# Two strides of the third attention, the opening of a 30-step FFN, and the order and register loads of an expert stage

## The chip, the cores and the metric

The kernel runs on one core of a Trainium2 chip. The metric is the time of one execution on the device in microseconds (us), as the median of several runs. Five engines work side by side, each through its own list of instructions: PE (matrix products), DVE and POOL (elementwise, POOL also sends gathers and scatters), ACT (functions of one operand), and SP, which only issues transfers (DMA). Instructions wait for one another by semaphores.

## What is computed

The input x has 4096 rows of 256 values, adj is a 4096 x 4096 matrix of zeros and ones. Two layers follow one another, each a graph attention and then a network on the rows, with residual additions. Cut to what matters:

```python
# attention, 4 heads of 64; W, a1, a2 differ by layer
h = einsum('nd,mdo->mno', x, W)
e = leaky_relu((h @ a1)[:, :, None] + (h @ a2)[:, None, :], 0.2)
attn = softmax(where(adj > 0, e, -9e15))
out = elu(attn @ h)                      # heads side by side

# layer 0
x = x + attention(layernorm(x))                          # g0
def step(h):                                             # 30 times
    h = h + 0.01 * tanh(h)
    h = h * sigmoid(h)
    return layernorm(h) @ W.T + b
x = x + thirty_steps(layernorm(x))
# layer 1
x = x + attention(attention(layernorm(x)))               # g1, then g2
f = layernorm(x)
p = softmax(relu(f @ rw1 + rb1) @ rw2 + rb2)             # 6 experts
weights, which = softmax(top 2 of p), their numbers
expert(e) = relu(relu(f @ w1[e] + b1[e]) @ w2[e] + b2[e]) @ w3[e] + b3[e]
x = x + sum of weights * expert(which)
```

## The kernel before

A group is 4 tiles of 128 rows: 8 groups of 512 rows in all (G = 4, NG = 8). The stages follow one another; in the profiled execution g0 ends near 603 us, the FFN near 1627, g1 at 2109 and g2 at 2646, and then come the experts.

**Attention** (`attention`, from L161). A stage first prepares: it loads the rows by groups (`load`, L258; the four buffers `ring` are shared between stages through `load_ahead`, L90), transposes them (`columns`, L268), multiplies by the weights (`products`, L297), and splits the values h into a high and a low f16 half in `vals` (`upper`, L364, on ACT; `lower`, L382, on DVE). g2 takes its rows without normalising them; there POOL spreads the rows' sums `xt` over 128 columns (`xsb`, L431 and L432) as the left side of a product on PE. Then the main part runs over chunks of 8 tiles of rows, heads, and quarters of the other rows. `step_of` (L450) makes signs `st` by ACT (L464) or DVE (L462), and DVE makes two masks of them with the loaded mask `m` (L569, L575). PE multiplies each mask by a row of 130 values (L521, in `products`, L509). The list of DVE and ACT is written out by hand there. Sums are closed by `lower_sums` (L470), `whole_sums` (L476) and `close` (L480). The last argument of `attention`, `apart`, holds two strides in elements: from one row of values in `vals` to the next (f16), and between two sums in PSUM (f32, `apart_s`):

```python
acc[:, i, part * apart_s : part * apart_s + 2 * DV],
masked[part][:, at_i // TR, s, rows],
values[:, j, h, part],
```

DV is 65. g0 has (130, 130), g1 (160, 130), g2 (130, 256), set in the calls (L1011).

**FFN** (L828 to L982). A unit is one group in one of 30 steps, 240 units in all. `slot(at)` (L857) issues parts of several units: tanh (L907) on ACT and the addition (L908) on POOL of unit `at`; silu (L893), the f16 half (L897, ACT) and the other half (`lower`, L898, DVE) of unit `at` − 2, with a transposing DMA of both halves issued by SP; statistics (L917, L919) on DVE; transposes on PE and a copy (L924) of unit `at` − 3, its deviation (L927 on ACT, L928 on POOL); the products (L937, L940) of unit `at` − 4, and scaling (L877) by DVE of unit `at` − 5. The lists of PE, DVE, ACT and POOL are in the order in which the code issues them, SP's is not: a scheduler places its transfers. The table `opening` adds, in the first slots, the normalisation of the first rows: `measure` (L747, DVE), `rate` (L755: ACT, then POOL at L760, L762 and L763), and `init` (L774), which normalises a group either on ACT (L782) or, with its third argument True, on DVE (L779). From slot 32 on, the rows of the residual are loaded again, a group each 24 slots (`load` into `ring`, `load_apart` into `hold`, L835), since the last step adds them.

**Experts** (from L1018). The 4096 rows are treated as two halves. `route` (L1080) is a generator with six parts for one half: for each group statistics (`over_std`, L96: L101 and L103 on DVE, L105, and a power on POOL at L106), normalisation `n` (L1111, L1114), a store of `n` to `nd`, transposes (L1122), the router's product (L1101), its second product (L1131) and logits; then the two best experts; then the place of each row in a list sorted by expert, from which come `expert` (the expert's number of each of T = 37 tiles, L1240 to L1248), `source` and `dest` (L1250 to L1260; the sums by PE at L1231), the biases `bsel` (L1263 to L1273), and the weights of the two experts. Half 0 is routed ahead of the loop; after its first four parts the experts' weights `ew` (18 x 256 KB) and `b3` are loaded. The loop (L1419 on) takes the 74 tiles one after another: `gather` (L1312) fetches the rows by `source` four tiles ahead, `turn` transposes them (L1326, L1328), `fetch` (L1330) copies an expert's weights (L1346), `hidden` (L1348: products L1354, L1365 on ACT, L1367 on DVE) runs twice, `result` (L1369: products L1375, addition and scatter to `yd`, L1378). Half 1 is routed in parts between the tiles. `combine` (L1390) loads the results of a half and adds them, weighted, to `acc`, from where they are stored.

The number of the expert is an address in three engines. `fetch` reads it into registers of PE, DVE and ACT, for a few tiles at a time:

```python
n = min(4, T - t)
_, values = nc.values_load_multi_w_load_instructions(
    expert[h][0:1, t : t + n],
```

Of the kernel before, what the change touches and what calls it, by code (L numbers as in the profile page):

```python
# [11 lines left out]
F32 = mybir.dt.float32  # L12
# [6 lines left out]
OP = mybir.AluOpType  # L19
AX = mybir.AxisListType  # L20
# [3 lines left out]
P = 128  # L24
C = 256
KC = C // P
H = 4
D = C // H
E = 6
G = 4  # L30
# [4 lines left out]
DV = D + 1  # L35
# [11 lines left out]
def gnn_ffn_kernel(ctx: ExitStack, tc: tile.TileContext, a: dict, out: bass.AP):  # L47
# [34 lines left out]
    def rows_of(t, g):  # L82
        return t[g * GR : (g + 1) * GR, :].rearrange("(r p) c -> p r c", p=P)
# [6 lines left out]
    def load_ahead(src, g, view=rows_of, queue=nc.sync):  # L90
        t = ring[:, turns[0] % 4]
        turns[0] += 1
        queue.dma_start(t, view(src, g))
        ahead[g] = t

    def over_std(pool, src):  # L96

        st = pool.tile([P, G, 6], F32, name="ln_st")
        mv = pool.tile([P, G, 2], F32, name="ln_mv")
        for r in range(G):  # L100
            nc.vector.bn_stats(st[:, r, :], src[:, r, :])  # L101
        for r in range(G):
            nc.vector.bn_aggr(mv[:, r, :], st[:, r, :])  # L103
        rstd = pool.tile([P, G], F32, name="ln_rstd")
        nc.vector.tensor_scalar(rstd, mv[:, :, 1], EPS, None, op0=OP.add)  # L105
        nc.gpsimd.tensor_tensor(rstd, rstd, mhalf, OP.pow)  # L106
        return rstd, mv
# [53 lines left out]
    def attention(tag, src, norm, w, front, chunks, first, ends, following, side={}, apart=(2 * DV, 2 * DV)):  # L161
# [7 lines left out]
        with ExitStack() as scope:  # L169
# [68 lines left out]
            with ExitStack() as ps:  # L238
# [189 lines left out]
                if sums is None:  # L428
                    xt = prep.tile([P, KC], F32, name="xt")
                    nc.vector.tensor_reduce(xt, xs, axis=AX.X, op=OP.add)  # L430
                    xsb = prep.tile([P, KC, P], F32, name="xsb")  # L431
                    nc.gpsimd.tensor_copy(xsb, xt[:, :, None].to_broadcast([P, KC, P]))  # L432
                    pt = small_ps()
                    for k in range(KC):
                        nc.tensor.matmul(pt[:, :C], xsb[:, k, :], w[:, k, :C], start=(k == 0), stop=(k == KC - 1))
                nc.scalar.activation(
# [304 lines left out]

    def load(g, queue=nc.sync):
        if g not in ahead:
            load_ahead(x1d, g, queue=queue)
        x1[g] = ahead.pop(g)

    def measure(g):  # L747
# [79 lines left out]
    with ExitStack() as scope:  # L827
# [7 lines left out]
        def load_apart(src, g):  # L835
            x1[g] = hold.tile([P, G, C], F32, name="x1")
            nc.sync.dma_start(x1[g], rows_of(src, g))

        for g in range(4, NG):
# [5 lines left out]

        th, zs, mvs, rs, zT, zT16, pos = {}, {}, {}, {}, {}, {}, {}
        units = FFN_STEPS * NG
        opening = {
            0: [(init, 2)],
            1: [(rate, 4), (rate, 5), (init, 3, True)],  # L850
            2: [(init, 4, True)],
            3: [(init, 5, True), (measure, 6)],
            4: [(rate, 6), (measure, 7)],
            5: [(init, 6), (rate, 7)],
            6: [(init, 7)],
        }
        def slot(at):  # L857
            g, part = divmod(at - 4 * NG, 3 * NG)
            if 0 <= g < NG and part == 0:
                if g < NG // 2:  # L860
                    load(g)
                else:
                    load_apart(x1d, g)
            u = at - 3
# [26 lines left out]
            if 0 <= u < units:  # L891
                z = zs[u] = work.tile([P, G, C], F32, name="z")
                ins = nc.scalar.activation(z, th.pop(u), AF.Silu, scale=0.01)  # L893
                if not u:
                    follows(ins, closed[1], "one change of tables")
                z16 = work.tile([P, 2, G, P], F16, name="z16", bufs=4)
                nc.scalar.activation(z16[:, 0], z[:, :, P:], AF.Identity, scale=scale[:, :1])  # L897
                lower = nc.vector.scalar_tensor_tensor(  # L898
                    z16[:, 1], z[:, :, P:], scale[:, :1], z16[:, 0], op0=OP.mult, op1=OP.subtract
                )  # L900
                zT16[u] = work.tile([P, 2 * G, P], F16, name="zT16", bufs=4)
                nc.sync.dma_start_transpose(zT16[u], z16.rearrange("p s r c -> p (s r c)"))
# [83 lines left out]
    def runs_of(t, g):  # L986

        return t[g * GR : (g + 1) * GR, :].rearrange("(p r) c -> p r c", r=G)
# [11 lines left out]
    for n in range(2):  # L1000
# [10 lines left out]
            {} if n else side,  # L1011
            (2 * DV, 256) if n else (160, 2 * DV),
        )
# [7 lines left out]
    with ExitStack() as scope:  # L1021
# [3 lines left out]
        bT = one.tile([P, NB], F32, name="bT")  # L1025
        acc = one.tile([P, NT, C], F32, name="acc")
        ws = one.tile([P, 2, NT], F32, name="ws")
        bsel = [one.tile([P, T, 2 * KC], F32, name=f"bsel{h}") for h in range(2)]
        expert = [one.tile([P, T], I32, name=f"expert{h}") for h in range(2)]
        dest = [one.tile([P, T], I32, name=f"dest{h}") for h in range(2)]  # L1030
        source = [one.tile([P, T], I32, name=f"source{h}") for h in range(2)]
        ew = [one.tile([P, E, KC, C], F32, name=f"ew{i}") for i in range(3)]
        b3 = one.tile([P, E, C], F32, name="b3")
# [43 lines left out]
        def over(t, n=NTH, m=E):  # L1077
            return t[:, :, None].to_broadcast([P, n, m])

        def route(h, turned, bank):  # L1080

# [3 lines left out]
            def load(g):  # L1085
                if h * NGH + g not in ahead:
                    load_ahead(x3d, h * NGH + g, runs_of)
                rows[g] = ahead.pop(h * NGH + g)

            load(0)  # L1090
            load(1)
            for g in range(NGH + 2):
                if g + 2 < NGH:
                    load(g + 2)
                if g < NGH:
                    stds[g] = over_std(rwork, rows[g])
# [8 lines left out]
                if 1 <= g <= NGH:  # L1105
# [18 lines left out]
                    nc.scalar.activation(acc[:, at : at + G, :], t, AF.Identity, bias=mone)  # L1124
                    yield
                if 2 <= g:
                    u = g - 2
# [91 lines left out]
            for i in range(2):  # L1219
# [18 lines left out]
                yield  # L1238
            seen = rone.tile([P, T, E - 1], F32, name="seen")
            nc.vector.tensor_tensor(  # L1240
                seen,
                along[:, :T, None].to_broadcast([P, T, E - 1]),
                first[:, None, 1:].to_broadcast([P, T, E - 1]),
                OP.is_ge,
            )
            ex = rone.tile([P, T], F32, name="ex")
            nc.vector.tensor_reduce(ex, seen, axis=AX.X, op=OP.add)
            nc.vector.tensor_copy(expert[h], ex)  # L1248
            lst = rone.tile([P, T, 2], F32, name="lst")
# [10 lines left out]
            nc.vector.tensor_copy(dest[h], df)  # L1260
            yield
            ohe = rone.tile([P, T, E], F32, name="ohe")
            nc.vector.tensor_tensor(  # L1263
# [19 lines left out]
        with tc.tile_pool(name="r_ps", bufs=1, space=PSUM) as psum, tc.tile_pool(  # L1283
# [7 lines left out]
            nc.tensor.transpose(ps[:, :NB], br, ident[:NB, :NB])  # L1291
            nc.vector.tensor_copy(bT, ps[:, :NB])
            steps = route(0, turned, bank)
            for _ in range(4):
                next(steps)
            for i in range(3):
# [3 lines left out]
            nc.sync.dma_start(b3, bcast_rows(a["L1_ffn_expert_b3"]))  # L1300
            for _ in steps:
                pass

# [26 lines left out]
        def fetch(i):  # L1330

            h, t = divmod(i, T)
            if i not in which:
                n = min(4, T - t)
                _, values = nc.values_load_multi_w_load_instructions(
# [135 lines left out]
```

## Time and profile before

| | us |
|---|---|
| median of 3 runs | 2967.96 (2966.99 to 2968.54) |
| the profiled execution | 2983.79 |
| its span | 2982.0 |
| PE busy in the span | 2795.9 (94%) |
| DVE busy | 2737.1 (92%) |
| ACT busy | 2463.9 (83%) |
| POOL busy | 1159.1 (39%) |

All durations come from the one profiled execution, whose time stands beside the median. A row of the groups gives a line of the code, its engine and operation, what it writes and reads, the shapes, the number of instructions; then the busy time in us and the mean of one in ns; then the engine's idle time just ahead of such instructions and what ended most of it. In a timeline each row is a start, a duration, the engine, the line and the operation; x4 stands for four in a row, and brackets hold the idle time before it. The clock in the windows is the share of full speed that PE was granted.

### The profile page before, as it was taken

The page shows a single profiled execution, that of the slowest core. Times are in us where ns is not written, and L with a number is a line of the kernel's source. Part 1 is how long each engine was busy: PE and PEld are TensorE (multiplying, and loading weights), DVE is VectorE, ACT ScalarE, POOL GpSimd, SP SyncE. Part 2 cuts the span into 40 slices and gives each one's busy share as a digit, 9 for nine tenths or more (in the row PEclk, how much of TensorE's full clock was granted, in tenths as well). Part 3 has the DMA queues.
Part 4 walks back from the last instruction along what each step waited for, and adds up shares of the span by engine and source line. Part 5 has one row for each costly group of instructions (what it writes and reads, how often), then busy time and mean ns, then how long its engine had stood idle before and what let it go on. Part 6 is the DMA issues. An engine that isn't in the chain of part 4 may idle for free. (4 is left out here: it accounts for less than half of the span.)

```text
span 2982.0 us, 82665 instructions
## 1 busy us (share of the span) xinstructions
PE 2795.9 (94%) x33923; PEld 2553.5 (86%) x33923; DVE 2737.1 (92%) x5769; ACT 2463.9 (83%) x3125; POOL 1159.1 (39%) x1084
## 2 busy tenths in 40 slices
PE   7899999979999999999998999999899999977986
PEld 5799999968888888888887999999799999967885
DVE  7999999999999999999998899999889999976665
ACT  5799999978888888888877999999799999954332
POOL 3000000079999999999982000000300000015563
PEclk9999999989999999999999999999999999988998
DMA  9999885043333333333353032120302222142243
GB/s 281 274 258 242 230 234 159 25 126 69 68 69 68 68 67 70 68 67 70 68 110 119 26 99 72 49 87 27 108 27 94 66 94 94 31 141 93 79 165 133
DMA packets 484450, 320.07 MB, mean 107 GB/s; under 512 B 416589, under 2 KB 445418, under 8 KB 477930
## 3 DMA queue, kind: packets, MB, share of 16 engines
q1 hardware_dynamic: 474034, 290.27, 36.1%
q0 software_dynamic: 7104, 19.41, 2.1%
q8 instruction: 268, 4.39, 0.6%
q10 hardware_dynamic: 2936, 5.11, 0.5%
q14 instruction: 108, 0.88, 0.1%
HBM read 183.00 MB, written 52.04 MB: 79 GB/s over the span
## 5 line engine op out<-in xcount | busy, mean ns | idle before, releaser
L521 PE MATMUL acc<-vals,st 128*128 128x130 f16 x12288 | 1425.1, 219 | 39.0 <-DVE u L476 30.6
L521 PE MATMUL acc<-vals,below 128*128 128x130 f16 x12288 | 1424.7, 221 | 14.0 <-DVE below L575 13.2
L464 ACT ACTIVATE st<-f1b,nf 128x1024 int8<-128x1024 f32 x1265 | 1334.2, 1145 | 30.3 <-PE acc L521 19.8
L521 PEld LDWEIGHTS <-below 128*128 128x128 fp8e4 x12288 | 1185.9, 97 | 55.0 <-issue 42.6
L521 PEld LDWEIGHTS <-st 128*128 128x128 fp8e4 x12288 | 1207.2, 98 | 9.6 <-DVE st L569 7.8
L937 PE MATMUL po<-wT,zT 128*128 128x256 f32 x1920 | 576.2, 382 | 6.1 <-DVE y L877 3.5
L940 PE MATMUL po<-w,zT 128*128 128x256 f16 x3840 | 577.9, 273 | 0.5 <-DMA zT<-z 0.5
L908 POOL TENSOR_TENSOR th<-th,y 128x1024 f32<-128x1024 f32 x232 | 548.9, 2366 | 14.5 <-DVE z_st L917 0.4
L940 PEld LDWEIGHTS <-zT 128*128 128x128 f16 x3840 | 376.6, 98 | 161.7 <-DMA zT<-z 1.2
L575 DVE TENSOR_TENSOR below<-m,st 128x1024 int32<-128x1024 int32 x384 | 469.9, 1224 | 32.6 <-DVE st L569 0.9
L569 DVE TENSOR_TENSOR st<-st,m 128x1024 int32<-128x1024 int32 x384 | 466.8, 1216 | 0.2
L877 DVE SCALAR_TENSOR_TENSOR y<-po,z_rs,bias 128x256 f32<-128x256 f32 x928 | 384.3, 476 | 2.2 <-PE tp L869 0.7
L917 DVE BATCH_NORM_STATS2 z_st<-z 128x6 f32<-128x256 f32 x960 | 335.5, 412 | 0.0
L937 PEld LDWEIGHTS po<-wT,zT 128*128 128x128 f32 x1920 | 291.1, 192 | 15.6 <-issue 3.7
L893 ACT ACTIVATE z<-th 128x1024 f32<-128x1024 f32 x240 | 251.9, 1050 | 17.6 <-POOL th L908 16.8
L928 POOL TENSOR_TENSOR z_rs<-z_rs,mhalf 128x4 f32<-128x4 f32 x240 | 245.4, 1022 | 3.1 <-ACT z_rs L927 3.1
L907 ACT ACTIVATE th<-y 128x1024 f32<-128x1024 f32 x232 | 241.7, 1042 | 0.0
L924 ACT COPY zT<-tp 128x512 f32<-128x512 f32 x240 | 140.4, 585 | 90.6 <-PE tp L869 89.5
L462 DVE TENSOR_SCALAR st<-f1b,nf 128x1024 int8<-128x1024 f32 x271 | 201.0, 742 | 6.2 <-PE acc L521 6.2
L760 POOL TENSOR_TENSOR x_rs<-x_rs,mhalf 128x4 f32<-128x4 f32 x8 | 9.4, 1175 | 505.3 <-ACT x_rs L759 505.3
L1046 POOL IOTA along_i<- 128x512 int32 (+1 forms) x5 | 2.8, 557 | 485.8 <-PE acc L521 485.7
L439 POOL MEMSET hs<- 128x4 f32 x3 | 0.3, 103 | 485.9 <-DVE u L493 485.9
(263 smaller groups left out, 3158.5 us busy)
## 6 DMA issues: line engine op xcount, KB each, us to landing
ring<-in_adj_dram SPq DMA_DIRECT2D x64, 1024.0 KB
m<-edges SPq DMA_DIRECT2D x32, 1024.0 KB
f1b<-fd SPq DMA_DIRECT2D x48, 512.0 KB
edges<-m SPq DMA_DIRECT2D x16, 1024.0 KB
y<-yd SPq DMA_DIRECT2D x16, 512.0 KB
ew<-in_L_ffn_expert_w_dram SPq DMA_DIRECT2D x18, 256.0 KB
t<-in_x_dram SPq DMA_DIRECT2D x8, 512.0 KB
old<-in_x_dram SPq DMA_DIRECT2D x16, 256.0 KB
```

Of the source, the lines that this page charges most:

```text
L464: nc.scalar.activation(out, f1, AF.Sign, bias=f2, scale=-1.0)
L521: nc.tensor.matmul(acc[:, i, part * apart_s : part * apart_s + 2 * DV], masked[part][:, at_i // TR, s, rows], values[:, j, h, part], start ...
L569: nc.vector.tensor_tensor(above, above, whole, OP.bitwise_and)
L575: nc.vector.tensor_tensor(below, whole, above, OP.bitwise_xor)
L877: nc.vector.scalar_tensor_tensor(t[:, r, :] if end else y[:, g * G + r, :], po[:, r, :], rstd[:, r : r + 1], t[:, r, :] if end else bias, ...
L893: ins = nc.scalar.activation(z, th.pop(u), AF.Silu, scale=0.01)
L907: nc.scalar.activation(th[at], was, AF.Tanh, scale=0.01)
L908: ins = (nc.gpsimd if at else nc.vector).tensor_tensor(th[at], th[at], was, OP.add)
L917: nc.vector.bn_stats(st[:, r, :], z[:, r, :])
L928: nc.gpsimd.tensor_tensor(rs[u], rs[u], mhalf, OP.pow)
L937: nc.tensor.matmul(po[:, r, :], src[:, r * P : (r + 1) * P], wT, start=True, stop=False)
L940: nc.tensor.matmul(po[:, r, :], src16[:, part * G + r, :], w16[:, other, :], start=False, stop=(part == 1 and other == 1),)
```

## The change

It has six parts.

1. g2 gets the strides of g1, (160, 130). Its `xsb` is dropped: PE reads `xt` itself, spread by the access pattern.
2. In the FFN's opening, groups 4 and 5 are normalised on ACT, not on DVE, in slots 3 and 4; group 3 stays on DVE. The rates of groups 4 and 5 are issued in slot 0, not in slot 1.
3. The eight loads of rows for the residual each get a dependence on the latest `lower` (L898), so that the scheduler can't place them earlier.
4. In the experts' stage, the rows of half 1 are loaded straight into `acc`, the first two groups ahead of the weights, and the statistics of these two groups are issued within the routing of half 0. `expert` is worked out after `source` and `dest`. DVE's list in the routing of half 0 is in the order of the code.
5. `ew` is allocated in the reverse order, ahead of `acc` and `ws`.
6. An expert's numbers are read in three loads for each half: 4, 17 and 16 tiles; before there were ten.

The diff, cut to its core:

```diff
@@ over_std, attention, load
-    def over_std(pool, src):
+    def over_std(pool, src, mark=""):
...
-                    xsb = prep.tile([P, KC, P], F32, name="xsb")
-                    nc.gpsimd.tensor_copy(xsb, xt[:, :, None].to_broadcast([P, KC, P]))
                     pt = small_ps()
                     for k in range(KC):
-                        nc.tensor.matmul(pt[:, :C], xsb[:, k, :], w[:, k, :C], start=(k == 0), stop=(k == KC - 1))
+                        nc.tensor.matmul(
+                            pt[:, :C], xt[:, k : k + 1].to_broadcast([P, P]), w[:, k, :C], start=(k == 0), stop=(k == KC - 1)
+                        )
@@ the FFN
+        halved = []
         opening = {
-            0: [(init, 2)],
-            1: [(rate, 4), (rate, 5), (init, 3, True)],
-            2: [(init, 4, True)],
-            3: [(init, 5, True), (measure, 6)],
-            4: [(rate, 6), (measure, 7)],
-            5: [(init, 6), (rate, 7)],
+            0: [(init, 2), (rate, 4), (rate, 5)],
+            1: [(init, 3, True)],
+            3: [(init, 4), (measure, 6)],
+            4: [(rate, 6), (init, 5), (measure, 7)],
+            5: [(rate, 7), (init, 6)],
             6: [(init, 7)],
         }
...
-                if g < NG // 2:
-                    load(g)
-                else:
-                    load_apart(x1d, g)
+                ins = load(g) if g < NG // 2 else load_apart(x1d, g)
+                follows(ins, halved[0], "in mid-stage, when the queue has room")
...
+                halved[:] = [lower]
@@ the call for g1 and g2
-            (2 * DV, 256) if n else (160, 2 * DV),
+            (160, 2 * DV),
@@ the experts
-        acc = one.tile([P, NT, C], F32, name="acc")
-        ws = one.tile([P, 2, NT], F32, name="ws")
...
-        ew = [one.tile([P, E, KC, C], F32, name=f"ew{i}") for i in range(3)]
+        ew = [one.tile([P, E, KC, C], F32, name=f"ew{i}") for i in (2, 1, 0)][::-1]
+        acc = one.tile([P, NT, C], F32, name="acc")
+        ws = one.tile([P, 2, NT], F32, name="ws")
...
+        early = {}
+
+        def rest(g):
+            return acc[:, (NGH + g) * G : (NGH + g + 1) * G, :]
+
+        def measure_other(g):
+            early[g] = over_std(rone, rest(g), f"_{g}")
@@ route
             def load(g):
-                if h * NGH + g not in ahead:
-                    load_ahead(x3d, h * NGH + g, runs_of)
-                rows[g] = ahead.pop(h * NGH + g)
+                if h:
+                    rows[g] = rest(g)
+                    if g in early:
+                        stds[g] = early.pop(g)
+                    else:
+                        nc.sync.dma_start(rows[g], runs_of(x3d, NGH + g))
+                else:
+                    rows[g] = ahead.pop(g)
...
-                if g < NGH:
+                if g < NGH and g not in stds:
                     stds[g] = over_std(rwork, rows[g])
...
+                if not h and g >= NGH:
+                    measure_other(g - NGH)
...
-            seen = rone.tile([P, T, E - 1], F32, name="seen")
-            nc.vector.tensor_tensor(
-                seen,
-                along[:, :T, None].to_broadcast([P, T, E - 1]),
-                first[:, None, 1:].to_broadcast([P, T, E - 1]),
-                OP.is_ge,
-            )
-            ex = rone.tile([P, T], F32, name="ex")
-            nc.vector.tensor_reduce(ex, seen, axis=AX.X, op=OP.add)
-            nc.vector.tensor_copy(expert[h], ex)
             lst = rone.tile([P, T, 2], F32, name="lst")
...
             nc.vector.tensor_scalar(source[h], sf, float(NH - 1), None, op0=OP.min)
             nc.vector.tensor_copy(dest[h], df)
             yield
+            seen = rone.tile([P, T, E - 1], F32, name="seen")
+            nc.vector.tensor_tensor(
+                seen,
+                along[:, :T, None].to_broadcast([P, T, E - 1]),
+                first[:, None, 1:].to_broadcast([P, T, E - 1]),
+                OP.is_ge,
+            )
+            ex = rone.tile([P, T], F32, name="ex")
+            nc.vector.tensor_reduce(ex, seen, axis=AX.X, op=OP.add)
+            nc.vector.tensor_copy(expert[h], ex)
@@ around route(0)
+            for g in range(2):
+                nc.sync.dma_start(rest(g), runs_of(x3d, NGH + g))
             steps = route(0, turned, bank)
-            for _ in range(4):
-                next(steps)
+            with tc.manual_schedule(engines={mybir.EngineType.DVE}):
+                for _ in range(4):
+                    next(steps)
...
-            for _ in steps:
-                pass
+            with tc.manual_schedule(engines={mybir.EngineType.DVE}):
+                for _ in steps:
+                    pass
@@ fetch
-                n = min(4, T - t)
+                n = 4 if t == 0 else min(-(-(T - 4) // 2), T - t)
```

## The prediction

> **What bounds the kernel now.** I read the page first, for the costliest groups and the slices; then busy time by windows, to cut the span into stages; then, in each stage that the change touches, the timeline and the waits. The edits lie in four places: the third attention (g2), the opening of the FFN (603 to 650 us), the head of the experts' stage (2646 to 2704 us) and its loop (2704 to 2957 us).
>
> ```profile
> L521 PE MATMUL acc<-vals,st 128*128 128x130 f16 x12288 | 1425.1, 219 | 39.0 <-DVE u L476 30.6
> ```
>
> The attentions are bound by PE: a row of this kind stands twice, and only 39.0 us of idle time precede 1425 us of work. Cut by attention (g0, g1, g2 in order; columns: window, its length, PE busy and matmuls, PEld busy, clock, DMA share, GB/s):
>
> ```profile
> 100.00:600.00 500.00, 476.52 (x8108) 471.07 (x8106) 0.99 0.72 198
> 1640.00:2105.00 465.00, 458.13 (x8030) 455.57 (x8028) 1.00 0.18 58
> 2170.00:2640.00 470.00, 465.61 (x8037) 463.65 (x8035) 1.00 0.21 65
> ```
>
> A matmul takes 458.13/8030 = 57.05 ns in g1 and 465.61/8037 = 57.93 ns in g2, at the same clock, shape and type. What differs in the code between the two is the pair of strides, and g2's masks and values lie elsewhere.
>
> In the FFN DVE sets the pace, 3.8 us per unit from 646 us on (37.99 busy of 38). In its opening DVE normalises rows:
>
> ```profile
> 610.66 0.69 DVE L628 SCALAR_TENSOR_TENSOR e<-e,u 128x512 f32<-128x512 f32 x1
> 611.46 3.42 DVE L779 TENSOR_SCALAR ring<-ring,x_rs,x_nm 128x256 f32<-128x256 f32 x4
> ...
> 617.05 3.37 DVE L779 TENSOR_SCALAR x<-x,x_rs,x_nm 128x256 f32<-128x256 f32 x4
> ```
>
> Four of these operations take 3.4 us here, while POOL adds (L908, below); the same shape at L1114 takes 0.41 each.
>
> ```profile
> 614.04 1.08 POOL L760 TENSOR_TENSOR x_rs<-x_rs,mhalf 128x4 f32<-128x4 f32 x1
> ...
> 617.49 2.47 POOL L908 TENSOR_TENSOR th<-th,ring 128x1024 f32<-128x1024 f32 x1
> ```
>
> In the head DVE works without a break from the logits to `source`, and PE waits:
>
> ```profile
> 2684.20 0.25 DVE L1201 TENSOR_TENSOR at__45084<-ps_s,shift 128x96 f32<-128x96 f32 x1
> ...
> 2685.72 1.07 DVE L1267 TENSOR_TENSOR sel<-ohe,bT 128x888 f32<-128x888 f32 x1
> ...
> 2688.70 0.77 DVE L1221 TENSOR_TENSOR ohh<-along,hi 128x592 f32<-128x592 f16 x1
> ...
> 2694.04 1.40 DVE L101 BATCH_NORM_STATS2 ln_st<-ring 128x6 f32<-128x256 f32 x4
> 2695.36 0.22 DVE L1250 COPY lst<-ps_r 128x74 f32<-128x74 f32 x1
> ...
> 2697.09 0.17 DVE L1259 TENSOR_SCALAR source<-sf 128x37 int32<-128x37 f32 x1
> ```
>
> The gather that needs `source` then stands behind one more operation of POOL:
>
> ```profile
> 2696.88 1.01 POOL L106 TENSOR_TENSOR ln_rstd<-ln_rstd,mhalf 128x4 f32<-128x4 f32 x1 [33.16 <-DVE sf L1258]
> 2698.15 1.54 POOL L1315 DMA_INDIRECT gx<-nd,source  x1 [0.26 <-DVE ln_mv L103]
> ```
>
> After that PE leads (window, length, PE busy, PEld, DVE, ACT, POOL, clock, DMA share, GB/s):
>
> ```profile
> 2640.00:2704.00 64.00, 29.00 (x236) 21.13 (x234) 43.84 (x159) 19.14 (x28) 19.85 (x38) 0.71 0.52 179
> 2704.00:2860.00 156.00, 148.77 (x1084) 136.60 (x1083) 101.99 (x321) 62.34 (x147) 92.32 (x92) 0.98 0.33 110
> ```
>
> **The change, part by part.** The sums are against the profiled run: 2983.79 us, a span of 2982.0 and 1.8 around it. It is 15.8 above the median of 2967.96; I carry the difference in us over to the median unchanged.
>
> *Strides of g2.* They become those of g1. By the busy times the gain is 0.88 ns x 8192 matmuls = 7.2 us; by the starts of g1's and g2's matmuls outside stalls (57.6 against 56.7 ns) it is 7.9. A stage with shorter matmuls waits a little longer for DVE's `u` (L476): 0.58 us per head in g1, 0.53 in g2, over 16 heads about 1 us back. Net −7. From first to last matmul g1 took 480.87 and g2 485.11, so that −4.2 is what remains if all of g1's stalls come along. Neither DVE (439 of 470 us) nor ACT (438) is the next bound. g0, with its values at 130 and its accumulators at 130, has matmuls of 58.8 ns: it is the values' stride that counts. [...]
>
> *Before g2.* The copy on POOL (L432) goes: PE's product at that place waits for ACT's L349, not for the copy, so 0. The masks load earlier, and two more sign steps (L464, 1.15 us each) fall on ACT, which is idle for 2 us before 2133 and full after it: 0 to +1, taken +0.5.
>
> *FFN opening.* Groups 4 and 5 go from DVE (3.37 and 2.10 us) to ACT (L782: 2.06 us each), and their two rates on POOL go ahead of the first add. In before these rates (614.04 to 617.49) hold up the add of unit 2 and ACT waits 2.45 us for it. From 612 to 646 us ACT is busy for 25.50 of 34, so that 4.1 more fit, but not in each step: a unit's 3.66 plus 2.06 is above DVE's 3.8 in the two steps concerned. `lower` (L898) of the first eight units starts at 614.80, 620.35, 626.23, 631.57, 636.71, 641.99, 645.80 and 649.60. Following both engines through these steps with the durations above, I get 642.9 instead of 645.80 for the seventh: −2.9. Bounds: −5.5 (all of DVE's two terms) and 0 (ACT takes it all back).
>
> *Rows in mid-stage.* Eight loads of 512 KB now wait for the latest `lower`; in before the scheduler had sent them during the opening. On SP's queue the transposes of z16 stand behind them. A transpose is used some 3.5 us after it has landed, which covers a load of 1.5 to 2 us ahead of it: 0. Without that cover it costs at most 8 x 0.5 = +4; from below −0.5, as L940 waits 0.46 us for zT in the opening.
>
> *Head.* Three things come before the first product of an expert (2704.33). (1) POOL's tables no longer wait for PE's last matmul of g2, so the first L106 starts about 1 us earlier, and from there to the logits PE and ACT form a chain: −1. (2) `seen` to `bsel` and the first copy of weights lie between 2684.20 and 2688.70; without them that stretch is about 2.3 us, dependent operations included: −2.2. One copy (0.33) and three of the four statistics of L101 (1.0) go from the stretch before `lst`, but the four n of group 4 (L1114, 1.35) come into it: 0. (3) L106 no longer precedes the first gather: −0.6. Against this PE now has transposes and the router's product of group 4 between the last L1231 and the first gathered tile, about 4.5 us at this clock with waits for ACT, where the window is 5 to 6 us: +0.4. Experts' numbers are cast 1.4 us after `source`, and `sel`, `bsel` come after; DVE is through with them 4.5 us after `source`, the first tile arrives at about the same time: 0. Net −3.4, between −6 and −1.
>
> *Moved out of the loop.* That work of group 4, 8 transposes (1.06 us) and a product (1.73), stood in PE's stream after 2704: −2.7, between −2.8 and 0 (if DVE or ACT is late next, as in the waits of about 1 us that PE has three times near 2859, 2873 and 2887).
>
> *Register loads.* 20 become 6 on each of PE, DVE and ACT.
>
> ```profile
> L1335 PEldq TENSOR_LOAD <-expert x20: 312/332/519, 2685.6 to 2945.3; - x20
> ```
>
> 14 x 0.33 us on PE's sequencer are 4.6 if nothing hid them. PE loses 0.3 us after about five of them, and the three waits of 1 us fall on loads of DVE (2858.5, 2872.6, 2886.7): 1.5 plus a third of 3 gives −2.5, from −5 to 0. The stops of 1.2 us every 15.5 us (2902, 2918, 2933) fall on no register load, and stay.
>
> Sum: −7 + 0.5 − 2.9 + 0 − 3.4 − 2.7 − 2.5 = −18.0. Profiled 2965.8, median 2950.0.
>
> **The rivals.** *The loop takes it back*: after the head PE waits for DVE, ACT and the stops, so that (3) to the register loads bring nothing. For it: in 2704 to 2860 PE is busy for 148.77 of 156, with waits between. Against it: these 7 us are spread over several causes. −7 + 0.5 − 2.9 = −9.4: 2958.5.
> *The stride is not the cause*: the 0.88 ns come from where g2's masks and values lie, and go on. [...] Against it: g0 behaves like g2 and shares only the stride with it. −18 + 7 = −11: 2957.
> *More than the sum*: the head reaches −6, the opening −5, registers −5: 2941.
> *Slower*: statistics (L101) and n (L1114) of half 1 now stand in DVE's stream ahead of `source`, and read rows that are loaded in the head. If these land late, DVE halts, and `source`, all gathers and all experts move by as much, one for one. They are needed at about 2692; ahead of the last are 6.6 MB, at 179 GB/s 37 us after 2647, which is 2684. Every us past 2692 costs one; from 2710 the gain is gone, from 2716 the kernel is measurably slower. That needs about half the rate: 2975.
> *The change doesn't do what it says*: the compiled order shows each moved instruction where the diff wants it, so this is only left for the mid-stage loads, and is worth nothing there.
>
> **How the numbers follow.** The sum as it stands 0.50 (2944 to 2956); the loop takes it back 0.17; the stride brings nothing 0.15; more than the sum 0.08; several of these losses together, within 0.2% of before (5.9 us, about what can be told from no change), 0.05; slower 0.05. Faster than 2962.0: 0.50 + 0.08 + most of 0.32, 0.87 in all; the same 0.08; slower 0.05. Range: 2940 to 2962; below it lie 0.04, above it 0.13.
>
> **What would show it.** Right: g2's matmuls at 57.05 ns in the windows' view and g2 about 7 us shorter from first to last; the seventh `lower` of the FFN about 2.9 us earlier, measured from its first; the first expert's product about 54.7 us after the start of g2's last matmul (before: 2704.33 − 2646.21 = 58.1); fewer stops at register loads, and a loop from there to the last product about 5 us shorter. Wrong: g2 still at 57.9 ns, an idle DVE before L101 or `source`, idle PE before L940 in mid-stage, or ACT full in the opening with `lower` no earlier.

## The result, and the profile after

| | before | changed |
|---|---|---|
| median of 8 runs each | 2967.01 us (2964.83 to 2968.54) | 2957.99 us (2952.86 to 2962.11) |
| ratio, with its interval | | 0.9969 (0.9960 to 0.9978) |
| profiled execution, span | 2983.79, 2982.0 | 2957.77, 2955.8 |

The change saves 9.0 us. I had forecast 18.0. The profile of before is not one to subtract from: its execution took 17 us more than the median of its runs, while that of the changed kernel lies at its median. The runs below come in three groups, each on a chip of its own, and they differ in the same way: before took 2981.72 us in the first group (25 runs) and 2967.29 and 2967.63 us in the other two. The difference of 26 us between the two spans therefore mixes two things, and times are compared below only with the runs of before in the same group.

The stages of the table agree from chip to chip to 1 or 2 us, but for the loop of the experts. Not in the table is g0, which no part of the change touches: from its first L521 to its last it took between 503.7 and 508.0 us in the profiles, so that 2 us of a difference between two spans can be of its making. I cut the executions by starts of instructions (us): the FFN's opening from the last L521 of g0 to the seventh `lower`; the head from the last L521 of g2 to the first product of an expert; the loop from there to PE's last product. Before again is the first run below; its loop varies by 2.4 us between the two executions, the other rows by 0.2 or less.

| | before (first profile) | before again | changed | forecast of the difference |
|---|---|---|---|---|
| FFN opening | 42.9 | 42.9 | 39.3 | −2.9 |
| FFN from there to the last `lower` | 910.8 | 910.8 | 910.8 | 0 |
| transition to g2 | 52.4 | 52.4 | 54.1 | +0.5 |
| g2, first to last L521 | 485.1 | 485.1 | 479.0 | −7 |
| head | 58.1 | 58.3 | 54.7 | −3.4 |
| loop | 251.3 | 248.9 | 240.1 | −5.2 |

Up to the loop the forecast holds, but for the transition (+1.7). The loop's row can't be read: 240.1 looks better than forecast, but run 6 shows that the loop of before takes 236.1 us on another chip. In g2 a matmul now takes what it takes in g1; the windows of the changed kernel (window, length, PE busy, PEld busy, clock, DMA share, GB/s), g1 and then g2:

```profile
1640.00:2100.00 460.00, 453.14 (x7942) 450.57 (x7940) 1.00 0.19 60
2165.00:2630.00 465.00, 460.50 (x8065) 457.92 (x8064) 1.00 0.22 66
```

453.14/7942 is 57.06 ns and 460.50/8065 is 57.10 ns, where g2 had 57.93. The row of all three stages falls from 1425.1 to 1418.0 us, its idle time stays at 39.0:

```profile
L521 PE MATMUL acc<-vals,st 128*128 128x130 f16 x12288 | 1418.0, 220 | 39.0 <-DVE u L476 30.5
```

In the FFN's opening the two normalisations are on ACT, each behind a unit's own five operations, and one on DVE is left (timelines of the changed kernel):

```profile
607.97 3.42 DVE L779 TENSOR_SCALAR ring<-ring,x_rs,x_nm 128x256 f32<-128x256 f32 x4
```

```profile
613.95 2.06 ACT L782 ACTIVATE x<-x,x_nm,x_rs 128x256 f32<-128x256 f32 x4
...
619.60 2.06 ACT L782 ACTIVATE x<-x,x_nm,x_rs 128x256 f32<-128x256 f32 x4
```

The head, on DVE, POOL and PE:

```profile
2671.55 0.26 DVE L1215 TENSOR_TENSOR at__45115<-ps_s,shift 128x96 f32<-128x96 f32 x1
...
2673.57 0.77 DVE L1235 TENSOR_TENSOR ohh<-along,hi 128x592 f32<-128x592 f16 x1
...
2680.52 0.24 DVE L1254 COPY lst<-ps_r 128x74 f32<-128x74 f32 x1
...
2682.46 0.15 DVE L1263 TENSOR_SCALAR source<-sf 128x37 int32<-128x37 f32 x1
```

```profile
2683.50 1.24 POOL L1333 DMA_INDIRECT gx<-nd,source  x1 [20.98 <-DVE n L1126]
```

```profile
2689.66 1.92 PE L1372 MATMUL ph<-xT,w 128*128 128x128 f32 x8
```

From g2's last L521 to `at_` it is 36.6 us (38.0 before), from `at_` to `source` 10.9 (12.9), from `source` to the gather 1.04 (1.06), from there to the first product 6.2 (6.2).

What the forecast has wrong is what it made of a row that it used itself. The register loads of the changed kernel (minimum, median and maximum in ns):

```profile
L1353 ACTq TENSOR_LOAD <-expert x6: 317/1708/3580, 2684.2 to 2875.3; - x6
L1353 DVEq TENSOR_LOAD <-expert x6: 358/1357/3845, 2684.3 to 2876.3; - x6
L1353 PEldq TENSOR_LOAD <-expert x6: 343/1416/4142, 2684.3 to 2874.5; - x6
```

There are 6 instead of 20, but they take up to 4.1 us each instead of 0.33 (PEldq is the profile's row for PE's sequencer). One by one, on PE: 0.53 and 0.34 for the loads of 4 values, 1.38 and 1.45 for those of 17, 4.05 and 4.14 for those of 16. That is 11.9 us of sequencer time where before had 7.0. At the first load of 16 PE runs dry:

```profile
2766.13 0.38 PE L1344 MATMUL pt<-ident,gx 128*128 128x128 f32 x2
2769.49 1.84 PE L1372 MATMUL ph<-h,w 128*128 128x128 f32 x8 [2.98 <-issue]
```

Its load ran from 2765.4 to 2769.4 on PE, from 2763.6 to 2767.0 on ACT and from 2765.5 to 2769.2 on DVE: all three sequencers are held by loads of the same values. The eight products after it take 1.84 us; eight like them took 1.05 just before. The clock was granted at 0.86 over these 12 us, and at 0.53 from 2769.5 to 2772.9. At the second load of 16 PE stood for 1.63 us, and the clock stayed at 1.00 (changed kernel, the two stretches with a load of 16):

```profile
2764.00:2776.00 12.00, 9.02 (x55) 8.03 (x55) 6.91 (x18) 2.86 (x8) 6.86 (x6) 0.86 0.17 55
...
2872.00:2884.00 12.00, 10.37 (x81) 9.72 (x80) 5.88 (x18) 4.41 (x12) 7.24 (x7) 1.00 0.22 79
```

### The profile page after: what moved, and what is told of

The parts are those of the page before. It is cut to its first block, busy times and chain, and to the rows that moved or that the text cites. A ratio compares the mean times of both kernels' runs of the same rounds, so it can differ in the third digit from the quotient of the medians.

```text
span 2955.8 us, 82630 instructions
## 1 busy us (share of the span) xinstructions
PE 2787.5 (94%) x33923; PEld 2546.3 (86%) x33923; DVE 2735.0 (93%) x5761; ACT 2466.8 (83%) x3133; POOL 1158.4 (39%) x1083
## 5 line engine op out<-in xcount | busy, mean ns | idle before, releaser
L521 PE MATMUL acc<-vals,st 128*128 128x130 f16 x12288 | 1418.0, 220 | 39.0 <-DVE u L476 30.5
L521 PE MATMUL acc<-vals,below 128*128 128x130 f16 x12288 | 1417.6, 221 | 12.9 <-DVE below L575 12.0
L521 PEld LDWEIGHTS <-below 128*128 128x128 fp8e4 x12288 | 1194.6, 97 | 54.6 <-issue 48.0
L521 PEld LDWEIGHTS <-st 128*128 128x128 fp8e4 x12288 | 1205.9, 98 | 9.3 <-DVE st L569 7.5
L907 POOL TENSOR_TENSOR th<-th,y 128x1024 f32<-128x1024 f32 x232 | 549.0, 2367 | 14.6 <-issue 0.2
```

Source lines behind the costliest of these rows:

```text
L521: nc.tensor.matmul(acc[:, i, part * apart_s : part * apart_s + 2 * DV], masked[part][:, at_i // TR, s, rows], values[:, j, h, part], start ...
L907: ins = (nc.gpsimd if at else nc.vector).tensor_tensor(th[at], th[at], was, OP.add)
```

## The experiments

My theory after this was: the six large register loads cost time, the rest of the change is worth what was forecast or more. The rivals: the early rows and the new order of the head cost it back in the loop; or the experts' parts bring nothing at all, and the two profiles differ by their chips alone. The first four runs are one group, the next four another, the last four a third. Each is stated against the runs of before in its group.

**1. Before, unchanged.**

> The kernel before, unchanged, to see how its stages stand in an execution of ordinary time. Its profiled execution took 2983.79 us where the median of its runs is 2967; of the change the profile shows 26 us and the median 9. Theory A (the excess of 16 us of that one execution lies in the loop of the experts and in g0, which vary from execution to execution): this profile has a span near 2965, the loop from the first product L1354 to the last L1375 near 243 us instead of 251.3, the FFN and g2 as before (FFN from L521 to L521 1024.9, g2 485.1 us). Theory B (it is spread over all stages): each stage is shorter by 0.5%. Theory C (profiling costs it): the profile is near 2982 again.

Measured: 2981.53 us beside 2981.72, ratio 1.0002 (0.9993 to 1.0012); span of the profile 2977.6. None of the three theories as I put them: the profile is near 2982 again, and so are all timed runs of this group. So it isn't the profiling. It goes with the group, and by the record each group has its own chip; chip and occasion aren't parted by it. The run gives the column "before again" above.

**2. The strides of g2 alone** (without `xsb`, whose place the longer values need).

```diff
-            (2 * DV, 256) if n else (160, 2 * DV),
+            (160, 2 * DV),
```

> The kernel before with part 1 alone: the strides (160, 130) in g2 and no xsb, which makes the room for the longer values. My theory: g2 from its first to its last matmul 479 us instead of 485.1, at 57.05 ns a matmul in the windows, the transition before it up to 2 us longer; time 4 to 6 us below before. The rival, that g2's addresses or something else of the change shortened it: g2 stays at 485 and the time the same.

Measured: 2974.79 us, −6.9; ratio 0.9977 (0.9967 to 0.9987). g2 takes 478.7 us, the transition 54.8: −6.4 and +2.4 in the profile. The interval of the time is 3.9 to 9.8 us; within it the strides bring what was forecast, by themselves. The addresses of `vals` and of the masks move with the stride, and both strides were changed in one: the time alone can't part them.

The records of single matmuls, in the profiles that were there already, part them further. A row of `vals` has two bytes to a value, and the two masks `st` and `below` go with rows 0 and 1 in turn. At a stride of 130 values the rows for `st` begin at multiples of 8 bytes (from the start of `vals`), those for `below` 4 bytes past one; at 160 all begin at multiples of 16. The matmuls of L521 (duration in ns, minimum, median and maximum): g0 and g2 of before, then g2 of the changed kernel:

```profile
L521 PE MATMUL acc<-vals,below x4054: 220/221/315, 99.7 to 599.9; 128*128 128x130 f16 x194
L521 PE MATMUL acc<-vals,st x4054: 217/218/315, 99.8 to 600.0; 128*128 128x130 f16 x194
...
L521 PE MATMUL acc<-vals,below x3932: 220/221/222, 2169.8 to 2629.9; 128*128 128x130 f16 x197
L521 PE MATMUL acc<-vals,st x3931: 217/218/219, 2169.9 to 2629.9; 128*128 128x130 f16 x197
...
L521 PE MATMUL acc<-vals,st x3992: 217/220/221, 2169.8 to 2630.0; 128*128 128x130 f16 x200
L521 PE MATMUL acc<-vals,below x3991: 217/220/221, 2169.9 to 2629.9; 128*128 128x130 f16 x200
```

From start to start, outside stalls, it is 55.8 ns after a product with `st` and 59.4 after one with `below` in g2 of before, and 56.7 on average in g2 of the changed kernel. g0 has g1's stride of sums and g2's of values, and it alternates as g2 does (55.9 and 59.5 ns): the stride of the sums is not the cause. In both stages with a stride of 130 the slower product is the one whose row begins 4 bytes past a multiple of 8. That the beginning makes the difference was not shown: no run moved it and nothing else.

**3. The changed kernel with ten register loads for each half.**

```diff
-                n = 4 if t == 0 else min(-(-(T - 4) // 2), T - t)
+                n = min(4, T - t)
```

> The changed kernel with part 6 alone undone: an expert's numbers again in ten loads for each half. My theory: about 2.5 us slower than the changed kernel, 2960.5, with small losses of PE (0.3 us) at the loads in the loop. The rival, that the loop gained 11 us by the register loads: 2966 to 2969, the loop from 240 to 250 us. The other, that the register loads cost nothing: 2958.

Measured: 2970.20 us, −11.5; ratio 0.9963 (0.9950 to 0.9977), head 54.2, loop 249.4. My absolute numbers were for the other kind of chip. Against the ratio of the whole change (0.9969) it tells nothing yet; the ninth run repeats it. Beside run 2 and the opening (6.9 and 3.8) little is left for the early rows and the order on this chip: the head is 4.1 us shorter than in before again, but the loop isn't shorter at all (249.4 against 248.9).

**4. Before with the experts' parts (4, 5 and 6).** The code from L1018 on is that of the changed kernel, with the new argument of `over_std`; all ahead of it is before.

> The kernel before with the experts' parts of the change (4, 5 and 6) and nothing else. If the parts add up as in the two profiles (head 3.4, loop 11.2): 14 us below before, 2953. If they are worth what I forecast (8.6): 2958. If the loop takes it back, as one of my rivals has it: 0 to 3 us below before, with the head 3.4 us shorter and the loop as long as before's ordinary execution.

Measured: 2987.52 us, 5.8 slower; ratio 1.0023 (1.0014 to 1.0032). The head is 2.7 us shorter than in before again (55.6), the loop 6.3 longer (255.2). None of my three numbers: it is worse than the rival that I had written down. So the experts' parts together cost time here, and the cost is in the loop.

**5. The changed kernel, again.** No edit.

> The changed kernel, unchanged, on the same chip as the next three and beside the same runs of before. It tells what the register loads do against the run with ten loads. In the profile of the changed kernel a load of 17 values holds PE's sequencer for 1.4 us and one of 16 for 4.1, against 0.33 for 4 values, so that six loads take 11.9 us of PE's sequencer where twenty took 6.8. Theory A (cost grows with the values, and fewer loads bring nothing): ratio to before 0.9965, within 3 us of the run with ten loads. Theory B (three loads are worth the 9 us by which the two profiles' loops differ): ratio 0.994.

Measured: 2958.46 us, −8.8; ratio 0.9971 (0.9960 to 0.9983). This is the first result again, and theory B falls: three loads bring nothing. Head 53.8 and loop 243.2: the loop of one and the same kernel differs by 3 us between two profiles.

**6. The changed kernel with the experts' stage of before.** The code from L1018 on is that of before.

> The changed kernel with the experts' parts (4, 5 and 6) undone: strides, opening, mid-stage loads. The profiles of the two give -6.1 for g2, -3.6 for the opening and +2 for the transition. If these are what stays: 7.5 to 8 us below before, a ratio of 0.9974, about the same as the whole change, so that the experts' parts bring next to nothing in all. If the experts' parts bring their 8.6 us: the whole change is 8.6 us faster than this.

Measured: 2956.27 us, −11.0; ratio 0.9965 (0.9952 to 0.9979). The strides (6.9) and the opening (42.9 to 39.1, 3.8) make 10.7 of it. It is not slower than the whole change, which fits run 4. Its loop, the code of before on this chip, takes 236.1 us, where before again had 248.9: the chips differ by some 13 us there. PE's list is the same in both. PE stands idle for 4.7 us of this loop and for 14.7 us of the other, with the same twenty loads; the stops on "issue" that the forecast saw near 2902 and 2918 are not there.

**7. Run 4 with ten loads.** The edit of run 3, made to run 4.

> The kernel before with the order and the early rows of the experts (parts 4 and 5), but ten register loads as before. The same with three loads was 6 us slower than before, with its loop at 255.2 us and its head 2.7 us shorter. If the large loads are the cost: this run is 3 us or more faster than before, its loop 249 us. If the order of the head costs in the loop, for instance by instructions that come at other places: slower than before again, loop at 253 or more.

Measured: 2960.34 us, −7.0; ratio 0.9978 (0.9969 to 0.9987); head 55.3, loop 233.9. With runs 4 and 6 this parts the experts' stage: early rows and order give −7.0, where I had forecast 3.4 + 2.7 = 6.1. Beside the profile of run 6 the loop has 236.1 − 233.9 = 2.2 of it and the head 1.2. Another 2.7 us lie in g0 (503.7 against 506.4), where the two kernels don't differ, so that the experts' parts may be worth only some 4 of the 7; no profile of before is from this chip. The loads of part 6 turn that into a loss. The rival that blames the new order falls on this chip; on that of run 3 the order brought nothing in the loop.

**8. Loads of 4, 8, 8, 8, 8 and 1 values.**

```diff
-                n = 4 if t == 0 else min(-(-(T - 4) // 2), T - t)
+                n = 4 if t == 0 else min(8, T - t)
```

> The changed kernel with loads of 4, 8, 8, 8, 8 and 1 values for each half. If a load's time grows with its values from a fixed part (0.33 for 4, 1.4 for 17): 0.65 us for 8, 0.33 us more than for 4, and no time of the kernel changes by over 2 us. If large loads are what costs and each up to 8 values is hidden: 3 us faster than the changed kernel.

Measured: 2959.31 us, −8.0; ratio 0.9971 (0.9961 to 0.9982), loop 240.3. A load of 8 takes 0.59 us, near the 0.65 of the first alternative:

```profile
L1353 PEldq TENSOR_LOAD <-expert x12: 309/592/707, 2685.0 to 2920.6; - x12
```

The loop is 6.8 us longer than with ten loads (233.5 in run 9), although no load of PE takes over 0.71 us. With other loads the scheduler arranges DVE's list in another way, and puts a sum of `combine` ahead of an expert's activation, where it waits for its rows:

```profile
2828.00 0.88 DVE L1422 SCALAR_TENSOR_TENSOR acc<-y,ws,acc 128x256 f32<-128x256 f32 x2 [3.00 <-DMA y<-yd]
2828.79 0.60 DVE L1385 TENSOR_SCALAR h<-ph,bsel 128x128 f32<-128x128 f32 x2
```

PE waits 2.4 us for that h, and 2.1 us for another one near 2856; in the stretches of about 3 us that follow the clock is granted at 0.50 and 0.57. What loads of 8 cost without this is left open.

**9. The edit of run 3 once more.**

> The changed kernel with ten register loads for each half (part 6 undone), once more, beside the next three and the same runs of before. Head and loop together were 303.6 us on one chip, where before had 307.2 and before with three loads and the new order 310.8; on another chip the new order with ten loads had 289.2, with three 297.0. If large loads cost 6 to 8 us: 15 to 17 us faster than before on a chip where the whole change brings 9, a ratio near 0.9945. If the run on the first chip stands for it: 11 us, 0.9963.

Measured: 2949.73 us, −17.9; ratio 0.9941 (0.9927 to 0.9954); loop 233.5, head 53.9. The interval lies clear of that of the whole change in run 5. The same two stretches as above, in this kernel:

```profile
2764.00:2776.00 12.00, 12.00 (x94) 11.59 (x93) 8.18 (x24) 4.98 (x12) 8.63 (x9) 1.00 0.31 100
2872.00:2884.00 12.00, 12.00 (x95) 11.59 (x94) 7.74 (x22) 5.37 (x14) 8.68 (x10) 1.00 0.30 94
```

PE starts 94 and 95 matmuls where the changed kernel starts 55 and 81: 39/94 x 12 = 5.0 us and 14/95 x 12 = 1.8 us. Together this estimate has 6.8 us, as much as the loops of these two profiles differ by (240.1 − 233.5 = 6.5); runs 9 and 5 differ by 9.1 in time. The lists differ too: some 6% of PE's and a third of DVE's instructions from the head on stand at other places. In run 3, on the slower chip, the same kernel gained 11.5; why that chip's loop is longer wasn't tried.

**10. Before with part 6 alone.** The edit of `fetch` in the change, made to before.

> The kernel before with part 6 alone: three register loads for each half. My forecast for this step was -2.5 us, between -5 and 0. What the other runs say: +6 to +8, a ratio of 1.002 to 1.0027, with a sequencer held for about 4 us at the last load of each half on PE, DVE and ACT. If the large loads cost only together with the new order of the head: no change.

Measured: 2977.86 us, 10.2 slower; ratio 1.0036 (1.0023 to 1.0048). The loads take 1.4 and 4.1 us here too. PE stops on "issue" for 3.7 and 2.0 us at the two loads of 16. It is more than I expected, and the scheduler moves other work as well: the transposes and the router's products of group 4, which wait for DVE, now stand in PE's list ahead of the first gathered tile:

```profile
2697.03 1.64 PE L1122 MATMUL tp<-ident,n 128*128 128x128 f32 x4 [3.39 <-DVE n L1114]
...
2700.32 1.92 PE L1101 MATMUL ps<-fT,g_w 128*128 128x512 f32 x2
...
2705.77 1.14 PE L1354 MATMUL ph<-xT,w 128*128 128x128 f32 x8
```

The head takes 61.5 us, the loop 242.0; the experts' stage of before in run 6, on another chip, had 56.4 and 236.1. By this about half of the 10.2 us is in the head, ahead of the large loads' stops, and comes of the order of the lists.

**11. Loads of 4, 16 and 17 values** instead of 4, 17 and 16.

```diff
-                n = 4 if t == 0 else min(-(-(T - 4) // 2), T - t)
+                n = 4 if t == 0 else min((T - 4) // 2 if t == 4 else T, T - t)
```

> The changed kernel with loads of 4, 16 and 17 values for each half, instead of 4, 17 and 16. In the changed kernel the one of 17 takes 1.4 us and the one of 16, the last of the half, 4.1. If the place counts (the last load of a half, or the register count at that point): again about 1.3 and 4.1 in this order. If the size or the address counts: the last, with 17 values, differs from 4.1 by much. The kernel's time within 3 us of the changed kernel's in either case.

Measured: 2953.03 us, −14.6; ratio 0.9950 (0.9937 to 0.9964). The load of 16 takes 1.1 to 1.2 us on PE, the last one, of 17, takes 1.4 to 1.6; none takes 4:

```profile
L1353 PEldq TENSOR_LOAD <-expert x6: 343/1158/1577, 2684.1 to 2865.0; - x6
```

So neither the place in the half nor the number makes the 4.1 us. What is left is the first element (or the place and the number together): the slow load begins at element 21 of the list, these at 4 and 20.

The time gained by the swap, 14.6 − 8.8 = 5.8 us beside run 5, each against before in its own group, is far above the 3 us that I had allowed. This is the cleanest comparison for the loads: PE's and DVE's lists are those of the changed kernel but for a few instructions, and the six loads hold PE's sequencer for 6.1 us instead of 11.8. The intervals of the two ratios just touch; the loop takes 236.4 us, where the two profiles of the changed kernel have 240.1 and 243.2. Some 2 us may be g0's, which took 504.0 here and 506.0 in run 5.

**12. Loads of two values**, 19 for each half.

```diff
-                n = 4 if t == 0 else min(-(-(T - 4) // 2), T - t)
+                n = min(2, T - t)
```

> The changed kernel with 19 loads of two values (the last of one) for each half. If the fixed part of a load costs PE time (0.3 us each, not hidden): 18 more loads than with ten, 5 us slower than the run with ten. If small loads are hidden behind the queued matmuls, as at most of the ten: within 2 us of it, and faster than the changed kernel by 5.

Measured: 2949.39 us, −18.2; ratio 0.9940 (0.9927 to 0.9954), the same as ten loads.

```profile
L1353 PEldq TENSOR_LOAD <-expert x38: 308/539/2070, 2683.0 to 2912.2; - x38
```

Here 38 loads hold PE's sequencer for at least 38 x 0.54 = 20 us, three times as long as the twenty of before, and nothing is lost beside run 9, whose list for PE is almost the same. So it isn't the number of the loads, nor the sum of their times. With run 11 this points to the length of a single one.

## Why the prediction was right and wrong, point by point

The time lies in the range that I gave, above the value: half of the forecast gain came. That it lies in the range is owed to the range's width, which had room for other mechanisms than the one at work. One term of seven has the wrong sign, and the others, taken together, were a little too small.

- **Strides of g2, −7:** right; −6.9 in run 2, with −6.4 in g2 itself. In g2 of before the slower of the single matmuls are those with `below`, 59.4 ns against 55.8 from start to start; with the new strides the average is 56.7, where the two before have a mean of 57.6. The rival that the gain lies elsewhere falls as a forecast of the time; and g0, at other addresses and with the same stride of values as g2 had, shows the same alternation.
- **Before g2, +0.5:** too small. It is +0.7 to +2.4 in the runs with the new strides (53.1 to 54.8 against 52.4); run 7, with the old strides, has 53.3, so that not all of it is theirs. What makes two values of it wasn't followed.
- **FFN opening, −2.9:** right in kind and too small: −3.6 in the changed kernel's profile and −3.8 in the runs. It comes in another place than I had it: `lower` of the second unit follows the first after 2.26 us instead of 5.55, since no normalisation stands between them on DVE, and the next five intervals (5.71, 5.34, 4.97, 5.28, 3.80 us) are within 0.2 of those of before. There ACT takes back what DVE gains: it is busy for 27.16 of the 28 us from 612 to 640. **Mid-stage loads, 0:** right, 910.8 us in every profile.
- **Head, −3.4:** right in sum (58.1 to 54.7), by terms that cancel. The start is worth 1.4 instead of 1, DVE's list 2.0 instead of 2.2. (3) was wrong: L106 no longer precedes the gather, and the gather still starts 1.04 us after `source`, since by the profile it now waits for an n (L1126) next to it; and the 0.4 that I added for PE did not come.
- **Moved out of the loop, −2.7:** −2.2 between runs 6 and 7, each one profile; on the chip of run 3 nothing of it shows. Not settled.
- **Register loads, −2.5, from −5 to 0:** this is the step that failed. Measured: +10.2 alone (run 10), about half of it by the order of the lists, and +9 within the change (run 5 against run 9). I took 14 x 0.33 us as the time that goes, and let the six that stay cost the same 0.33, though the row is one for four values and they were to hold 16 and 17. And I closed the range at 0 for no reason. At that row's 0.33 us for four values, 0.083 for each, six loads of 74 values hold the sequencer, as an estimate, for as long as twenty of 74, 6.1 us in all, and nothing is to be gained; I had not weighed it. Measured are 7.0 us for the twenty and 11.9 for the six: a load of seventeen values took 1.4 us, as this estimate has it, but one of sixteen from element 21 took 4.1, three times as much.
- What I read in before as the price of its loads (PE's 0.3 us after five of them, three waits of 1 us) wasn't theirs: run 12 has twice as many and loses nothing, and in run 6, on another chip, the same twenty stand in a loop with 10 us less of idle PE.

Without part 6 my sum is −15.5 and the measured time −17.9 (run 9). The parts add up, as far as intervals of 4 us either way can show, and across groups: runs 6 and 7 give −11.0 and −7.0, together −18.0; with run 10's +10.2 that makes −7.8, and the change has −8.8 to −9.0.

Of the rivals, *the loop takes it back* named 2958.5, which is the measured time, by a mechanism that was not there: the head's gain and the moved work did come through, though not on every chip, and the register loads did not merely bring nothing. *Slower* did not happen; DVE never waits for the early rows ahead of `source`.

The version to keep is that of run 9: the changed kernel with ten loads for each half. It is 17.9 us faster than before there, and 11.5 on the slower chip (run 3). Run 12 is as fast.

## What to carry to other kernels

When instructions are merged, cost the one that is left at its own size: thirty-eight short ones (0.54 us each, run 12) behind queued work cost nothing here beside twenty (0.33 each, run 9), and one long one (4.1 us) that held three engines at once did cost. Of the two loads of 4.1 us in the changed kernel PE felt 2.98 and 1.63; for the rest it still had work. So look at the longest single piece, not at their sum alone. And where a scheduler orders the lists, a small edit in one place moves others: compare the lists, and run the part alone and the change without it before the sum is believed.

## What the runs showed of the hardware

The time of a register load (PE's sequencer, in us), by the number of its values and the first of them. Elements are counted from the start of a half's list; the first load of a run, and a few others that lasted longer (most of them in run 12), are left out:

| values, first element | measured |
|---|---|
| 1, 36 | 0.31 |
| 4, multiples of 4 | 0.33 |
| 2, even | 0.54 |
| 8, from 4 on | 0.59 to 0.61 |
| 16, from 4 | 1.12 to 1.20 |
| 17, from 4 or 20 | 1.36 to 1.58 |
| 16, from 21 | 3.9 to 4.2 |

Sixteen values from element 21 took over three times as long as sixteen from element 4. What makes the difference was not shown: no run moved the first element and nothing else.

After PE had stood for 3 us in the loop of the changed kernel, its next 8 products took 1.84 us instead of 1.05, with a clock of 0.53 for 3.4 us, so that this stop cost more than its length. Run 8 shows the same after stops of 2.4 and 2.1 us (0.50 and 0.57); after the stop of 1.63 us in the changed kernel the clock was 1.00. And the same loop, with the same list for PE, took 248.9 us on one chip and 236.1 on another, while g1 (480.9 to 481.5 us) and the FFN after its opening (910.8) agreed: a profile is compared with one from the same chip, or by stages that are known to agree.
